# Attention scores computed a second time with the keys on the partitions, the maximum added by a product, and the sums taken as extra columns of V

## The chip, the core and the metric

The kernel runs on one core of a Trainium2 chip. The metric is the device time of one execution in microseconds (us). The engines named below are TensorE (PE; its weight loads are listed apart as PEld), VectorE (DVE), ScalarE (ACT), GpSimd (POOL) and SyncE (SP, which only issues DMAs). They run side by side and wait for each other by semaphores. PE's results go to PSUM, which the kernel allots in eight banks of 512 f32 columns on 128 partitions; DVE and ACT take them from there to SBUF.

## What is computed

Four conditional layers run one after the other on `x`, 64 sequences of 64 tokens with 256 features. Layer 0 is a feed-forward layer with quantised activations and weights, layer 1 attention and a gated feed-forward layer, layer 2 a layer norm, layer 3 an adapter whose weights differ from sequence to sequence. The change concerns the attention of layer 1, with 16 heads of 16 features:

```python
def _attention(x, W_q, W_k, W_v, W_o):
    b, l, dm = x.shape
    d_head = dm // N_HEADS
    scale = sqrt(N_HEADS / dm)                     # 0.25
    q = split(x @ W_q.T); k = split(x @ W_k.T); v = split(x @ W_v.T)
    attn = jax.nn.softmax(scale * jnp.einsum('bnqd,bnkd->bnqk', q, k), axis=-1)
    o = jnp.einsum('bnqk,bnkd->bnqd', attn, v)
    o = o.transpose(0, 2, 1, 3).reshape(b, l, dm)
    return o @ W_o.T
...
a_alpha = (t @ attn_alpha_w.T)[:, None, :]
x = x + a_alpha * _attention(_ada_rmsnorm(x, t, attn_gamma_w, attn_beta_w), W_q, W_k, W_v, W_o)
```

## The kernel before

The 4096 tokens are worked on in eight blocks (`i`) of 512 tokens, that is eight sequences. Three stretches follow each other on PE: layer 0, the attention, and the feed-forward layer with layers 2 and 3. The order of instructions on PE, DVE, ACT and POOL is the order in which the program writes them (`tc.manual_schedule`); each engine works through its own in that order, and waits come from the data and from the rotation of buffers.

The attention is the loop `for w in range(W)` (L1070) with sixteen units. Unit `w` is half `tp = w % 2` of block `i = w // 2`: four sequences, all heads. PSUM is split there into one tile `S` of four banks and four single banks `mm`, which are used in rotation. The large f32 products are made of three products of high and low parts (`mm3`, L81 to L85, type f32r); `oh`, `ol` and `xh`, `xl` are such parts.

A unit does this with its scores:

- `a_score` (L637): 32 matmuls, one for each of two pairs of sequences (`u`), two halves of the features (`m`), four groups of 32 features (`j`) and two sequences of a pair (`h`). A group of 32 features is two heads. The weights are 64 queries of `qf`, the moving operand 128 columns of `kb`: the 64 keys twice, once with the odd head's features set to zero and once with the even head's. The result has the queries on the partitions and fills the four banks of `S`.
- `a_shift` (L655), twice, each on two banks: DVE takes the maximum over 64 keys (`mx`, L660) and subtracts it (L662), which moves the scores to SBUF (`ex`).
- `a_exp` (L665), twice: ACT's exponential, in place. `a_sum` (L669), twice: DVE sums the exponentials; `a_recip` (L673) takes the reciprocals `rz`.
- `a_turn` (L683), twice: sixteen 128x128 transposes on PE (L690) put the keys on the partitions; ACT copies the four banks to `pts` (L694), DVE one of them in odd units (L692). `a_rows` (L678): ACT spreads the reciprocals to 512 columns.
- In the next unit `a_weigh` (L697): 32 matmuls with 32 columns of `vb` as weights (two heads of 16, the other one's keys set to zero) and 64 columns of `pts` moving, four side by side; ACT copies the result (L713), PE turns the spread reciprocals (L716, four transposes), DVE multiplies (L717). `a_parts` (L720): ACT makes `oh`, POOL `ol`. `a_project` (L729): the product with `W_o`, then DVE, POOL and, once a block, a DMA of POOL's queue that stores `x2`.

Between these stand pieces for the blocks to come: `todo[0]` to `todo[2]` are two value products (`a_val`) and one key product (`a_qk`) of block `i + 1` in even units and three key or query products in odd ones; `a_norm_turn` turns the normed block `i + 2` (eight transposes in even units, L256); `a_scale`, `a_begin` and `a_load` norm and load later blocks; `splits.turn` splits weights of the feed-forward layer. In the last two units `f_keep` computes the first products of that layer, and `a_turn(W - 1, 1)` to `a_project(W - 1)` stand among its first steps, after PSUM has been divided anew.

`vb` is written by four DMAs a block from `vx`, whose zeros are set once at the start (L1014).

Of the kernel before, what the change touches and what calls it, by code (L numbers as in the profile page):

```python
# [17 lines left out]
P = 128  # L18
# [18 lines left out]
def tile_kernel(ctx: ExitStack, tc, xT, x, condT, cw, upT, downT, qkvT, woT, ghT, outT_w,  # L37
# [108 lines left out]
    def cond_load():  # L146
# [6 lines left out]
        cwt = crest["w"] = pools["kv"].tile([P, TT, 2, 8, 32], F32, tag="vb", bufs=2, name="cwt")[:, :2].rearrange("p a e h d -> p (a e) (h d)")  # L153
# [4 lines left out]
    def cond_rest():  # L158
# [8 lines left out]
        nc.vector.tensor_tensor(w2, vc[:, 1, :], vc[:, 1, :], ALU.mult)  # L167
        bo = crest["bo"]
# [427 lines left out]
    def a_val(i, tp):  # L596
# [15 lines left out]
        vb = kv.tile([P, TT, 2, 8, 32], F32, tag="vb", bufs=2, name=f"vb{i}")  # L612
# [24 lines left out]
    def a_score(w):  # L637
# [15 lines left out]
        units[w] = dict(pS=pS, ex=[], pts=[], mx=pool.tile([P, 2, 32], F32, tag="mx", bufs=2, name=f"mx{w}"))  # L653

    def a_shift(w, e):  # L655

        pool, U = pools["b"], units[w]
        sv = U["pS"][:, 2 * e:2 * e + 2].rearrange("p j (a l) -> p (j a) l", l=L)
        ms = U["mx"][:, 0, 16 * e:16 * e + 16]
        nc.vector.tensor_reduce(ms, sv, AX.X, ALU.max)  # L660
        ex = pool.tile([P, 16, L], F32, tag="ex2", bufs=2, name=f"ex{w}_{e}")
        nc.vector.tensor_tensor(ex, sv, ms.unsqueeze(2).broadcast_to([P, 16, L]), ALU.subtract)  # L662
        U["ex"].append(ex)

    def a_exp(w, e):  # L665
        ex = units[w]["ex"][e]
        nc.scalar.activation(ex, ex, AF.Exp, scale=0.25)

    def a_sum(w, e):  # L669
        pool, U = pools["b"], units[w]  # L670
        nc.vector.tensor_reduce(U["mx"][:, 1, 16 * e:16 * e + 16], U["ex"][e], AX.X, ALU.add)

    def a_recip(w):  # L673
        pool, U = pools["b"], units[w]
        rz = U["rz"] = pool.tile([P, 4, 4, 2], F32, tag="rz", bufs=2, name=f"rz{w}")
        nc.vector.reciprocal(rz, U["mx"][:, 1].rearrange("p (j a h) -> p a j h", j=4, h=2))

    def a_rows(w):  # L678

        rp = units[w]["rp"] = pools["b"].tile([P, 32, 16], F32, tag="rp", bufs=1, name=f"rp{w}")  # L680
        nc.scalar.copy(rp, units[w]["rz"].rearrange("p a j h -> p (a j h)").unsqueeze(2).broadcast_to([P, 32, 16]))

    def a_turn(w, e):  # L683
        U = units[w]
        pv = U["ex"][e].rearrange("p (b h) l -> p b (h l)", h=2)
        pt = pools["b"].tile([P, 2, 512], F32, tag="pts", bufs=2, name=f"pts{w}_{e}")
        for k in range(2):
            pT = bank("mm")
            for a in range(4):
                nc.tensor.transpose(pT[:, a * P:(a + 1) * P], pv[:, 4 * k + a], ident)  # L690
            if w % 2 == 1 and k == 1:
                nc.vector.tensor_copy(pt[:, k], pT)  # L692
            else:
                nc.scalar.copy(pt[:, k], pT)  # L694
        U["pts"].append(pt)

    def a_weigh(w):  # L697

        i, tp = w // 2, w % 2
        pool = pools["b"]  # L700
        U = units.pop(w)
        pts, rp = U["pts"], U["rp"]
        po, vb = bank("po"), ablk[i]["vb"]
        for u in range(2):
            for m in range(2):
                for h in range(2):
                    o = (2 * u + m) * P + h * 64
                    for j in range(4):
                        nc.tensor.matmul(po[32 * j:32 * (j + 1), o:o + 64],
                                         lhsT=vb[:, 2 * tp + u, h, 4 * m + j, :], rhs=pts[j // 2][:, j % 2, o:o + 64],  # L710
                                         start=True, stop=True, tile_position=(0, 32 * j))
# [576 lines left out]
```

## Time and profile before

| what | value |
|---|---|
| runs | 748.68, 748.94, 749.75 us; median 748.94 |
| profiled execution, time | 748.95 us |
| profiled execution, span of the core | 746.8 us |
| granted PE clock | 1.00 |
| busy in the span: PE, DVE, ACT, POOL | 734.7 (98%), 542.2 (73%), 405.6 (54%), 340.4 (46%) us |
| layer 0 (0 to 258.5 us): PE, DVE, ACT busy | 256.4, 200.3, 123.8 us |
| feed-forward and adapter (436.7 to 746.8 us): PE, DVE, ACT busy | 303.1, 184.5, 128.3 us |
| bytes read from HBM and written to it | 71.4 and 29.6 MB |

Some groups of the attention, with the mean time of one instruction:

| group | instructions | one |
|---|---|---|
| L660 maximum, DVE, 128x1024 to 128x16 | 32 | 1220 ns |
| L662 subtraction, DVE, 128x1024 | 32 | 1225 ns |
| L671 sum, DVE, 128x1024 to 128x16 | 32 | 1214 ns |
| L667 exponential, ACT, 128x1024 | 32 | 1065 ns |
| L694 copies of `pts`, ACT, 128x512 | 48 | 621 ns |
| L692 copies of `pts`, DVE, 128x512 | 16 | 659 ns |
| L681 spreading of reciprocals, ACT, 128x512 | 16 | 667 ns |
| L713 copy of the weighed values, ACT, 128x512 | 16 | 580 ns |
| L717 product with the reciprocals, DVE, 128x512 | 16 | 677 ns |

How to read it: times of matmuls are from start to the modelled end, and matmuls overlap, so the distance between starts says what one costs. `32*64 32x128` means 32 rows and 64 columns of weights, and 32 partitions with 128 columns moving. A line such as L83 is that of a helper; the tiles' names tell which product it is.

### The profile page before, as it was taken

What the parts mean: (1) busy time and instruction counts of PE and PEld (TensorE: products, weight loads), DVE (VectorE), ACT (ScalarE), POOL (GpSimd) and SP (SyncE); (2) the same over time, 40 slices, a digit from 0 to 9 for tenths busy, and PEclk for the clock granted to TensorE, in tenths of its full rate; (3) what the DMA queues carried; (4) which work ended last, traced back from release to release, by engine and by line L of the source; (5) the groups of instructions that cost most, each with busy time, mean ns of one, the idle gap of its engine ahead of it and who ended that gap; (6) DMA issues with size and microseconds to landing.
All of it is one profiled execution on the core that took longest, in us unless ns stands there. A gap on an engine that the chain in (4) does not pass through costs nothing.

```text
span 746.8 us, 17456 instructions
## 1 busy us (share of the span) xinstructions
PE 734.7 (98%) x7036; PEld 612.1 (82%) x7036; DVE 542.2 (73%) x843; ACT 405.6 (54%) x849; POOL 340.4 (46%) x359
## 2 busy tenths in 40 slices
PE   9999999999999999999999999999999999999997
PEld 8866766777686878888888888888888888888886
DVE  4998878867687698889888876646555555565676
ACT  5553445335435588998888674535253434434242
POOL 2123133133134426765655427464646464545292
PEclk9999999999999999999999999999999999999999
DMA  8897999999995866444655237623261709080821
GB/s 258 244 265 171 270 280 231 300 278 261 229 273 108 195 153 162 113 134 122 164 150 129 79 101 183 148 52 91 63 163 32 196 4 224 1 198 2 222 62 58
DMA packets 117456, 118.87 MB, mean 159 GB/s; under 512 B 39632, under 2 KB 101200, under 8 KB 117376
## 3 DMA queue, kind: packets, MB, share of 16 engines
q1 hardware_dynamic: 109232, 91.29, 49.6%
q0 software_dynamic: 7488, 25.37, 10.9%
q10 hardware_dynamic: 656, 1.11, 0.5%
q8 instruction: 55, 0.90, 0.5%
q14 instruction: 25, 0.20, 0.1%
HBM read 71.41 MB, written 29.56 MB: 135 GB/s over the span
## 4 chain that ended last, share of the span: by engine, by line
PE 61%; DVE 17%; ACT 11%; issue 5%; DMA 3%; POOL 2%; SPq 1%; DVEq 0%; ACTq 0%; POOLq 0%
PE mm L83 9%; PE mm L85 8%; PE mm L84 8%; PE gh L85 4%; PE gh L84 4%; PE gh L83 4%; PE mm L476 3%; PE mm L298 3%; PE acc L83 2%; DMA wu<-s2d 2%; PE S L649 2%; DVE sg L799 2%; PE acc L85 2%; PE acc L84 2%; ACT x L878 2%
## 5 line engine op out<-in xcount | busy, mean ns | idle before, releaser
L83 PE MATMUL mm<-up,xhl 128*128 128x512 f32 x240 | 97.2, 405 | 0.0
L83 PE MATMUL gh<-xhf,gh 128*128 128x512 f32 x244 | 95.2, 390 | 0.0
L85 PE MATMUL gh<-xhf,gh 128*128 128x512 f32 x244 | 95.2, 390 | 0.0
L84 PE MATMUL gh<-xlf,gh 128*128 128x512 f32 x244 | 95.1, 390 | 0.0
L85 PE MATMUL mm<-up,xll 128*128 128x512 f32 x240 | 93.9, 391 | 0.0
L84 PE MATMUL mm<-up,xhl 128*128 128x512 f32 x240 | 93.6, 390 | 0.0
L799 DVE TENSOR_TENSOR sg<-gh,sg 128x512 f32<-128x512 f32 x60 | 41.3, 688 | 70.7 <-ACT sg L796 37.9
L450 ACT ACTIVATE g<-mm,rs_l 128x512 f32<-128x512 f32 x64 | 43.8, 689 | 80.6 <-PE mm L85 48.1
L837 DVE TENSOR_TENSOR hlo<-sg,hhi 128x512 fp32r<-128x512 f32 x58 | 55.2, 951 | 30.4 <-ACT hhi L836 29.5
L836 ACT CAST hhi<-sg 128x512 fp32r<-128x512 f32 x58 | 36.0, 620 | 71.9 <-DVE sg L799 71.1
L83 PE MATMUL acc<-wout,hhi 128*128 128x256 f32 x248 | 71.9, 290 | 0.0
L85 PE MATMUL acc<-wout,hlo 128*128 128x256 f32 x248 | 69.5, 280 | 0.8 <-DVE hlo L834 0.6
L451 DVE SCALAR_TENSOR_TENSOR h<-mm,rs_l,g 128x512 f32<-128x512 f32 x64 | 46.4, 744 | 32.8 <-PE mm L85 29.7
L84 PE MATMUL acc<-wout,hhi 128*128 128x256 f32 x248 | 69.3, 279 | 0.0
L260 POOL TENSOR_TENSOR xg<-xg,cv 128x512 f32<-128x512 f32 x32 | 35.3, 1114 | 71.2 <-DVE xg L259 71.2
L83 PEld LDWEIGHTS mm<-up,xhl 128*128 128x128 f32 x240 | 45.1, 188 | 15.2 <-issue 2.4
L85 PEld LDWEIGHTS gh<-xhf,gh 128*128 128x128 f32 x244 | 45.8, 188 | 9.6
L85 PEld LDWEIGHTS mm<-up,xll 128*128 128x128 f32 x240 | 45.0, 188 | 10.1
L84 PEld LDWEIGHTS mm<-up,xhl 128*128 128x128 f32 x240 | 45.2, 188 | 8.5
L83 PEld LDWEIGHTS gh<-xhf,gh 128*128 128x128 f32 x244 | 45.8, 188 | 7.3
L84 PEld LDWEIGHTS gh<-xlf,gh 128*128 128x128 f32 x244 | 45.8, 188 | 7.3
L660 DVE TENSOR_REDUCE mx<-S 128x16 f32<-128x1024 f32 x32 | 39.0, 1220 | 17.3 <-PE S L649 17.3
(220 smaller groups left out, 1929.6 us busy)
## 6 DMA issues: line engine op xcount, KB each, us to landing
gt<-in_g SPq DMA_DIRECT2D x32, 512.0 KB, 9.1
rows<-alphad SPq DMA_DIRECT2D x48, 256.0 KB, 4.8
vb<-vx SPq DMA_DIRECT2D x32, 256.0 KB, 5.1
wd<-s1d SPq DMA_DIRECT2D x32, 256.0 KB, 6.2
wu<-s2d SPq DMA_DIRECT2D x32, 256.0 KB, 6.0
xt<-in_x SPq DMA_DIRECT2D x8, 512.0 KB, 7.6
s1d<-stgs POOLq DMA_DIRECT2D x16, 256.0 KB, 8.0
s1d<-stg POOLq DMA_DIRECT2D x16, 256.0 KB, 7.9
```

The costliest lines, as they stand in the source:

```text
L83: nc.tensor.matmul(out, lhsT=l[0], rhs=r[0], start=first, stop=False)
L84: nc.tensor.matmul(out, lhsT=l[0], rhs=r[1], start=False, stop=False)
L85: nc.tensor.matmul(out, lhsT=l[1], rhs=r[0], start=False, stop=last)
L260: nc.gpsimd.tensor_tensor(b3(xg), b3(xg), bc(vb, c, i), ALU.add)
L298: nc.tensor.matmul(pb[s][c * 64:(c + 1) * 64], lhsT=gl[h], rhs=gt[h, c * GC:(c + 1) * GC], start=True, stop=True, tile_position=(64 * s, 6 ...
L450: nc.scalar.activation(g, pg, AF.Gelu, scale=rs[:, t:t + 1])
L451: nc.vector.scalar_tensor_tensor(h[:, ch * 512:(ch + 1) * 512], pv, rs[:, t:t + 1], g, ALU.mult, ALU.mult)
L476: nc.tensor.matmul(py[:, :D], lhsT=qt[:, f, :], rhs=wq[:, f, :], start=f == 0, stop=f == 7)
L660: nc.vector.tensor_reduce(ms, sv, AX.X, ALU.max)
L799: nc.vector.tensor_tensor(sg, pv, sg, ALU.mult)
L836: nc.scalar.copy(h_hi, sg)
L837: nc.vector.tensor_tensor(h_lo, sg, h_hi.bitcast(F32), ALU.subtract)
```

## The change

The exponentials are no longer turned; the scores are computed again, already turned.

- After `a_score` and the two maxima, `a_cut` splits the 32 maxima of each query into three bf16 parts (`cuts`, 24 of 32 columns of each group used).
- `a_score_turned` uses the same operands with their roles exchanged: 128 columns of `kb` are the weights, 64 queries of `qf` move, and four row groups of 32 work side by side. It writes to a new tile of the tag `S`, of which there is one, so into the four banks that `a_score` filled.
- `a_max_turn` transposes `cuts` (one bf16 transpose) and DVE copies it to `mt`. The new `a_shift` adds the negative maxima to the turned scores by 16 bf16 matmuls with the constant `sel` (entries 0 and -1) as weights. They accumulate in the same banks.
- `a_exp` reads PSUM and writes `pts` itself.
- `vx` and `vb` get two more columns for each pair of heads, one with ones at the keys of the even head, one at those of the odd head. `a_weigh` has 64 columns of `pts` as weights and 34 columns of `vb` moving, two side by side; its result has the queries on the partitions, and columns 32 and 33 are the sums of the exponentials. `a_divide` takes their reciprocals and multiplies, in two halves. The new `a_turn` turns the finished output by four transposes; ACT makes `oh` and DVE (before: POOL) `ol`.
- In the loop `a_scale`, `load_rows` and `a_load` stand before `a_score`, `a_norm_turn` turns one half in each unit instead of both in even ones, the key products of odd units have another order, and `a_project` stands at the unit's end.
- `cond_rest` builds `sel` and a bf16 identity, and POOL sets the ones in `vx` and zeros in `cuts`.

```diff
+        keys_of = main.tile([P, 8, 5], F32, tag="st", bufs=2, name="keys_of")
+        nc.vector.tensor_reduce(keys_of[:, :, 0:4], ident.rearrange("p (j c k) -> p k j c", j=4, c=4)[:, :, :, 0:3], AX.X, ALU.add)
+        nc.vector.tensor_reduce(keys_of[:, :, 4], keys_of[:, :, 0:4], AX.X, ALU.add)
+        nc.vector.tensor_scalar(pools["sel"], keys_of[:, :, 4:5].broadcast_to([P, 8, L]), -1.0, None, ALU.mult)
+        nc.vector.tensor_copy(pools["identb"], ident)
...
+    def a_max(w, e):
+        U = units[w]
+        if e == 0:
+            U["mx"] = pools["b"].tile([P, 32], F32, tag="mx", bufs=2, name=f"mx{w}")
+        nc.vector.tensor_reduce(U["mx"][:, 16 * e:16 * e + 16],
+                                U["pS"][:, 2 * e:2 * e + 2].rearrange("p j (a l) -> p (j a) l", l=L), AX.X, ALU.max)
+
+    def a_cut(w):
         pool, U = pools["b"], units[w]
-        sv = U["pS"][:, 2 * e:2 * e + 2].rearrange("p j (a l) -> p (j a) l", l=L)
-        ms = U["mx"][:, 0, 16 * e:16 * e + 16]
-        nc.vector.tensor_reduce(ms, sv, AX.X, ALU.max)
-        ex = pool.tile([P, 16, L], F32, tag="ex2", bufs=2, name=f"ex{w}_{e}")
-        nc.vector.tensor_tensor(ex, sv, ms.unsqueeze(2).broadcast_to([P, 16, L]), ALU.subtract)
...
+        mx, cuts = U["mx"].rearrange("p (j k) -> p j k", k=8), pools["cuts"][w % 2]
+        left = pool.tile([P, 4, 8], F32, tag="left", bufs=2, name=f"left{w}")
+        nc.vector.tensor_copy(cuts[:, :, 0:8], mx)
+        nc.vector.tensor_tensor(left, mx, cuts[:, :, 0:8], ALU.subtract)
+        nc.vector.tensor_copy(cuts[:, :, 8:16], left)
+        nc.vector.tensor_tensor(cuts[:, :, 16:24], left, cuts[:, :, 8:16], ALU.subtract)
+
+    def a_score_turned(w):
         i, tp = w // 2, w % 2
+        qf, kb = ablk[i]["qf"], ablk[i]["kb"]
+        pt = units[w]["pt"] = banks("S", 4)
         for u in range(2):
             for m in range(2):
                 for h in range(2):
+                    b, o = 4 * tp + 2 * u + h, (2 * u + m) * P + h * 64
                     for j in range(4):
+                        js = slice(32 * j, 32 * (j + 1))
+                        nc.tensor.matmul(pt[:, j, o:o + 64], lhsT=kb[js, m, b].rearrange("p e l -> p (e l)"),
+                                         rhs=qf[js, m, b * L:(b + 1) * L], start=o == 0, stop=False,
+                                         tile_position=(32 * j, 0))
+
+    def a_max_turn(w):
+        U = units[w]
+        pm = bank("mm").bitcast(BF16)[:, :P]
+        nc.tensor.transpose(pm, pools["cuts"][w % 2].rearrange("p j k -> p (j k)"), pools["identb"])
+        mt = U["mt"] = pools["b"].tile([P, P], BF16, tag="mt", bufs=2, name=f"mt{w}")
+        return lambda: nc.vector.tensor_copy(mt, pm)
+
+    def a_shift(w):
+        U = units[w]
+        for a in range(4):
+            for j in range(4):
+                js = slice(32 * j, 32 * (j + 1))
+                nc.tensor.matmul(U["pt"][:, j, a * P:(a + 1) * P],
+                                 lhsT=pools["sel"][js, 2 * a:2 * a + 2].rearrange("p e l -> p (e l)"),
+                                 rhs=U["mt"][js], start=False, stop=a == 3, tile_position=(32 * j, 0))
+
+    def a_exp(w, e):
+        U = units[w]
+        pts = pools["b"].tile([P, 2, 512], F32, tag="pts", bufs=2, name=f"pts{w}_{e}")
+        nc.scalar.activation(pts, U["pt"][:, 2 * e:2 * e + 2], AF.Exp, scale=0.25)
+        U["pts"].append(pts)
+
+    def a_weigh(w):
+        i, tp = w // 2, w % 2
+        U, vb = units[w], ablk[i]["vb"]
+        U["po"] = []
+        for u in range(2):
+            po = bank("mm")[:, :16 * 17].rearrange("p (n d) -> p n d", d=34)
+            U["po"].append(po)
+            for m in range(2):
+                for j in range(4):
+                    for h in range(2):
+                        o = (2 * u + m) * P + h * 64
+                        nc.tensor.matmul(po[h * 64:(h + 1) * 64, 4 * m + j], lhsT=U["pts"][j // 2][:, j % 2, o:o + 64],
+                                         rhs=vb[:, 2 * tp + u, h, 4 * m + j], start=True, stop=True,
+                                         tile_position=(0, 64 * h))
+
+    def a_divide(w, u):
+        pool, U = pools["b"], units[w]
...
+        po, rz = U["po"][u], U["rz"][:, u]
+        nc.vector.reciprocal(rz, po[:, :, 32:34])
+        nc.vector.tensor_tensor(U["of"][:, u * D:(u + 1) * D].rearrange("p (n e d) -> p n e d", n=8, e=2),
+                                po[:, :, 0:32].rearrange("p n (e d) -> p n e d", e=2),
+                                rz.unsqueeze(3).broadcast_to([P, 8, 2, 16]), ALU.mult)
+
+    def a_turn(w):
...
+            nc.tensor.transpose(pr[:, a * P:(a + 1) * P], of[:, a * P:(a + 1) * P], ident)
...
+        nc.scalar.copy(oh, pr)
         units[w, "o"] = (oh, ol)
+        return lambda: nc.vector.tensor_tensor(ol, pr, oh.bitcast(F32), ALU.subtract)
...
+        a_score(w)
+        a_max(w, 0)
+        a_max(w, 1)
+        a_cut(w)
+        if w > 0:
+            a_weigh(w - 1)
+        todo[0]()
+        a_score_turned(w)
+        max_turned = a_max_turn(w)
+        if w > 0:
+            a_divide(w - 1, 0)
+        max_turned()
+        if w > 0:
+            a_divide(w - 1, 1)
+        turned = a_norm_turn(i + 2, tp) if i + 2 <= NBLK else lambda: None
+        a_shift(w)
         a_exp(w, 0)
         if w > 0:
+            low = a_turn(w - 1)
+            low()
+        a_exp(w, 1)
         todo[1]()
+        turned()
         todo[2]()
...
+        if w > 0:
+            a_project(w - 1)
```

## The prediction

> **What bounds the kernel now.** I read the busy time by stretch first, then the matmul engine's timeline over one attention unit, then the groups by shape for prices. A unit is one of the sixteen passes of the loop over `w`; it covers four of the 64 sequences. The attention stretch runs from the first score matmul at 258.5 us to about 436.7 us.
>
> ```profile
> core 0: us, PE busy (x) PEld busy (x) DVE busy (x) ACT busy (x) POOL busy (x), PEclk, DMA share, GB/s
> 258.50:436.70 178.20, 175.24 (x2990) 151.97 (x2989) 157.43 (x178) 153.46 (x313) 101.13 (x96) 1.00 0.52 135
> ```
>
> Columns: stretch, length, then busy time and instructions of PE, PEld, DVE, ACT and POOL. PE is idle for 178.20 - 175.24 = 2.96 us in sixteen units, DVE for 20.8 us and ACT for 24.7 us. Per unit that is 9.8 us of DVE and 9.6 us of ACT in 11.1 us. All three are nearly full, but PE is fullest, and a busy PE hides small waits, so its phases have to be read from starts. One unit of PE:
>
> ```profile
> 323.84 1.21 PE L649 MATMUL S<-kb,qf 32*64 32x128 f32 x64
> 324.98 1.10 PE L709 MATMUL mm<-pts,vb 128*32 128x64 f32 x64
> 326.01 0.66 PE L716 MATMUL mm<-ident,rp 128*128 128x128 f32 x4
> 326.42 0.37 PE L83 MATMUL mm<-wv,xha 128*128 128x256 f32 x1
> ...
> 329.24 0.39 PE L83 MATMUL mm<-xha,qk 128*128 128x512 f32 x1
> ...
> 330.62 1.39 PE L256 MATMUL mm<-ident,xna 128*128 128x128 f32 x8
> 331.90 0.39 PE L83 MATMUL mm<-wo,oh 128*128 128x256 f32 x1
> ...
> 333.38 1.47 PE L690 MATMUL mm<-ident,ex 128*128 128x128 f32 x12
> 335.01 0.66 PE L690 MATMUL mm<-ident,ex 128*128 128x128 f32 x4 [0.16 <-ACT pts L694]
> 335.60 1.21 PE L649 MATMUL S<-kb,qf 32*64 32x128 f32 x64
> ```
>
> Columns: start, merged length, engine, line, tiles, shape, count. Differences of starts give the phases: scores 1.14, weighing 1.03, turning the reciprocals 0.41, value products 2.82, one key product 1.39, norm turn 1.28, output projection 1.48, turning the exponentials 2.22; together 11.76. The next unit takes 10.42 (L649 again at 346.02), so a pair averages 11.09 a unit. Every phase follows the last at once. The reader is to see that whatever is added to PE here is added to the time.
>
> **Prices on PE.** An f32 product that is not a transpose is recorded twice, so the 32 score matmuls stand as x64. What a small matmul costs can be bound by its moving columns or by the load of its weights, and the rows tell these apart.
>
> ```profile
> 83.35 2.00 PE L176 MATMUL mm<-ct,cwt 64*128 64x64 f32 x28
> 85.28 0.65 PE L180 MATMUL mm<-cwt,ct 64*64 64x256 f32 x4
> ...
> 531.36 2.04 PE L943 MATMUL mm<-x,wd 128*64 128x64 f32 x64
> 533.22 1.10 PE L959 MATMUL mm<-dn,wu 128*64 128x64 f32 x32
> ```
>
> ```profile
> L176 PEld LDWEIGHTS mm<-ct,cwt 64*128 64x128 f32 x28 | 1.9, 188 | 0.4 <-ACT junkl L232 0.4
> L709 PEld LDWEIGHTS mm<-pts,vb 128*32 128x32 f32 x1024 | 15.6, 110 | 3.3 <-issue 1.9 <-ACT rp L681 1.0 <-ACT pts L694 0.4
> L943 PEld LDWEIGHTS mm<-x,wd 128*64 128x64 f32 x448 | 13.7, 138 | 0.5 <-issue 0.4
> L476 PEld LDWEIGHTS <-qt 128*128 128x128 bf16 x256 | 23.0, 98 | 8.9 <-issue 6.7
> ```
>
> - L709 (32 weight columns, four tiles side by side, 64 moving columns): 64 records are 16 steps in 1.03 us; the starts inside stand 56 ns apart, and about 0.13 is the change of tiling.
> - L943 (64 weight columns, two side by side, 64 moving): 32 steps in 533.22 - 531.36 = 1.86 us, 58 ns a step.
> - L176 (128 weight columns, 64 moving): six pairs of row halves and two single ones, two records each, are 16 steps in 1.93 us; the starts stand 112 ns apart. Same 64 moving columns, twice the step: with 128 columns the weight load sets the pace. The loads' own times, 110, 138 and 188 ns for 32, 64 and 128 columns, rise by about 0.8 ns a column and agree.
> - A 128x128 f32 transpose (L690, L716): 109 ns between starts.
> - A change of tiling: the last start of L649 to the first of L709 is 0.20 us, of L709 to L716 0.15; about 0.1 over the step itself.
>
> **The change on PE, per unit.**
> 1. *Exponentials' turn goes.* The L690 phases sum to 33.2 us, 2.08 a unit. About 0.09 of that is the change to score tiling, which stays: **-1.99**.
> 2. *Second scores* (`a_score_turned`): 32 f32 matmuls, 64 records, on four row groups of 32 rows, 128 weight columns, 64 moving: 16 steps. At L709's step 0.90, at L176's 1.79; it has L176's columns on both sides, so I take 1.79, plus 0.19 for going into the tiling and out: **+1.98** (low end 1.09).
> 3. *Weighing turned round*: weights are now 64 columns of `pts`, moving is 34 columns of `vb`, two tiles side by side: 32 steps. L943 has the same weights and gives 32 x 58 ns = 1.86, with 0.14 of tiling 2.00. Before it was 17.5/16 = 1.09 on average. **+0.91**; if the pace followed the moving columns instead, 34 of L943's 64 would be 31 ns a step, 1.13 in all, so about 0.
> 4. *Maximum's turn and the shift by a product*: one bf16 transpose (0.05 to 0.11, by L690), then 16 bf16 matmuls in 4 steps of 56 (L709) to 112 ns (L176), each with a change of tiling in and out. The bf16 weight load of L476 takes 98 ns against 188 for f32, so I take the lower step: 0.06 + 0.03 + 0.22 + 0.22 = **+0.53** (0.45 to 0.80).
> 5. *Norm turns* are four a unit instead of eight every second: 0.47 instead of 1.28/2: **-0.17**. The four transposes of the finished output replace the four of L716: 0.
>
> Sum **+1.26 us** a unit with PE alone.
>
> [...]
>
> **What lies beside PE.** DVE loses two subtractions (1.22 each), two sums (1.21), a reciprocal (0.34), the product with turned reciprocals (0.68) and one copy (0.66), 6.6 us a unit. It gains four operations of `a_cut` on 24 or 32 columns (0.15 to 0.34 each, by the 128x1 scalar operation L458 and the reciprocal L676; I take 0.2), the copy of `mt` (0.15 to 0.41, L458 and the 128x256 copy L183; 0.25), two reciprocals and two products of `a_divide` (0.2 and 0.42), and `ol` from POOL (0.69): 3.0. ACT loses three copies of `pts`, `rp` and `of`, 3.1 us, and gains nothing: the exponential keeps its 1.06 and reads PSUM. So DVE falls to 6.3 and ACT to 6.5 us a unit; none of it shortens a unit that PE fills. Priced at nothing for that reason: all of DVE's and ACT's relief, and POOL's loss of `ol` (1.29).
>
> New waits, counting from the first score of a unit. The two maxima end at 1.25 + 2.44 = 3.7, the cuts at 4.5. PE does weighing and the first todo until 1.14 + 2.00 + 1.41 = 4.55, so the second scores, which overwrite the same four banks, don't wait; without the weighing (w = 0) they wait 1.3. `max_turn` is at 6.5; its result, the copy on DVE (0.27 + 0.25 + 0.05 us later) is covered by the four norm transposes (0.47), which leaves about 0.1. `a_divide(w-1, 1)` stands behind that copy on DVE, and `a_turn`'s third transpose waits for it: 0 to 0.2. Exponentials and `oh` on ACT end 3.0 us after the shift, PE needs the banks 4.7 us after it. At the end of odd units the last `qf` copy is behind two exponentials, a copy and a cast on ACT and ends near the next score: 0 to 0.4 per pair. Together I take 0.15 a unit (0 to 0.6, the whole round trip of `mt` uncovered).
>
> SP's loads of `at` and `ax1` are issued some 2 us earlier, POOL's x2 store some 4 us later, both a block before use; they cost nothing, and if the store were late, `f_load` would be next. Outside the loop: five DVE operations in `cond_rest` (about 1.3 us where DVE is 77% busy) and three memsets on POOL, nothing on PE; if DVE's slack were gone there, up to 1.3.
>
> **Sum.** Fifteen units x (1.26 + 0.15) = 21.2. Unit 0 loses four norm turns and waits 1.3: -0.5. After unit 15 the FFN's banks wait for the last exponential, some 2 us of PE work against 3.0 on ACT: +1.0. Total +21.7 on the profiled run, whose span is 746.8 and time 748.95, beside a median of 748.94: **770.6 us**; for this case alone 767 (no new wait, item 4 at its low end: 15 x 1.18 + 0.5) to 775 (item 4 at its high end: 15 x 1.68 + 0.5).
>
> **Rivals.**
> - *The new chain of waits decides* (score, maxima, cut, turn, copy, shift): if 0.6 to 1.1 a unit stays uncovered, 15 x 0.45 to 0.95 more: 777 to 785. For it: DVE and PE now hand over three times inside a unit. Against: the slack worked out above.
> - *Loads hide behind neighbours, columns set the pace* (the faster side): items 2 and 3 at 1.09 and 0: per unit -0.54, total about -8, **741 us**. It begins to win where the two items together cost under 1.5 us a unit (1.99 + 0.17 - 0.53, less 0.15 of waits) instead of 2.89. For it: L709 keeps 56 ns with 64 moving columns. Against: L176.
> - *Half of that* (weighing by its 34 columns, second scores by their loads): +0.35 + 0.15 a unit, **757 us**. For it: L943 has as many moving as weight columns, so it can't tell which of them sets its step.
> - *DVE or ACT was the true bound*, so that their 3 us come back: PE's 2.96 us of idle in the stretch is all there is, -3; folded into the ranges.
>
> **Chances.** Forecast 0.60, chain of waits 0.16, half 0.12, columns alone 0.08, rest 0.04 (spread). The time is the forecast's. The range 756 to 783 leaves out the columns case and the far end of the chain. Under 0.2% (1.5 us) this kernel's runs, 748.68 to 749.75, can't be told from no change: faster 0.09, same 0.02, slower 0.89.
>
> **What would show it.** In the profile of the changed kernel: the second scores' phase near 2.0 us with starts 112 ns apart (1.1 refutes item 2); weighing near 2.0 us with 58 ns steps (1.1 refutes item 3); units of 12.4 to 12.6 us; DVE and ACT near 50% busy in the stretch while PE stays over 95%. PE idle over 0.5 us a unit ahead of the shift or of the output's turn would mean the chain decides. The prediction is wrong if loads of four row groups hide behind each other's products.

## The result, and the profile after

The changed kernel takes **779.6 us** (median of four runs, 777.8 to 782.2) beside 748.9 us (748.7 to 749.8): a ratio of 1.041, 95% interval 1.037 to 1.045. The forecast was 770.6 us in a range of 756 to 783. The sign and the mechanism held; the loss is 30.7 us where 21.7 were forecast.

The profiled execution of the changed kernel took 778.25 us, its span 776.5 (before 748.95 and 746.8). I cut both spans at the first score matmul of unit 0 and of unit 15, where the work is the same, and set the three parts beside the terms of the forecast:

| part of the span | before | after | difference | forecast |
|---|---|---|---|---|
| start to first score of unit 0 (layer 0) | 258.5 | 262.8 | +4.3 | 0, up to 1.3 |
| units 0 to 14 | 164.8 | 184.4 | +19.6 | 15 x 1.41 - 0.5 = +20.7 |
| first score of unit 15 to the end | 323.5 | 329.3 | +5.8 | +1.0 |
| sum | 746.8 | 776.5 | +29.7 | +21.7 |

Busy time by stretch, as in the prediction (stretch, length, then busy us and instructions of PE, PEld, DVE, ACT and POOL, the granted clock last but two); first the kernel before, cut at the same places:

```profile
core 0: us, PE busy (x) PEld busy (x) DVE busy (x) ACT busy (x) POOL busy (x), PEclk, DMA share, GB/s
258.50:423.30 164.80, 161.89 (x2743) 140.73 (x2742) 145.99 (x164) 144.14 (x299) 97.15 (x93) 1.00 0.51 130
```

and the changed kernel:

```profile
262.80:447.20 184.40, 183.14 (x3711) 161.10 (x3711) 100.94 (x204) 107.19 (x223) 79.05 (x80) 1.00 0.47 119
447.20:776.50 329.30, 321.19 (x2962) 283.57 (x2961) 194.56 (x308) 133.45 (x274) 169.81 (x145) 0.99 0.42 106
```

DVE falls from 146 to 101 us and ACT from 144 to 107, and none of it is to be seen in the time: PE is idle for 184.40 - 183.14 = 1.3 us in fifteen units. PE issues 3711 matmul records where it issued 2743. One unit of the changed kernel on PE's timeline, with the start first:

```profile
334.31 1.21 PE L654 MATMUL S<-kb,qf 32*64 32x128 f32 x64
335.44 2.06 PE L729 MATMUL mm<-vb,pts 128*64 128x34 f32 x64
337.44 0.38 PE L83 MATMUL mm<-wv,xha 128*128 128x256 f32 x1
...
339.04 2.01 PE L689 MATMUL S<-qf,kb 32*128 32x64 f32 x64
340.99 0.23 PE L697 MATMUL mm<-identb,cuts 128*128 128x128 bf16 x1
341.06 0.61 PE L261 MATMUL mm<-ident,xna 128*128 128x128 f32 x4
341.59 0.40 PE L707 MATMUL S<-mt,sel 32*128 32x128 bf16 x16
341.93 0.67 PE L750 MATMUL mm<-ident,of 128*128 128x128 f32 x4
...
346.72 0.55 PE L654 MATMUL S<-kb,qf 32*64 32x128 f32 x19
```

The phases by differences of starts: first scores 1.13, weighing 2.00, second scores 1.95, maximum's turn 0.07, norm turn 0.53, shift 0.34, output's turn 0.42. No phase waits for another engine. The unit takes 346.72 - 334.31 = 12.41 us; units 2 to 13 take 12.35 to 12.41, 12.39 on average, where the same units before averaged 11.04 (the pair that the prediction read, 11.09): 1.35 us more. Of this, 0.31 us falls on the products of the next block and the output projection, which themselves didn't change (5.96 us a unit instead of 5.65): the changes of tiling around the new phases come to stand in them (0.21 us from the last of the first piece's products to the second scores, where two such products stand 0.11 apart). Unit 14, which has no norm turn in either kernel, takes 13.75 us instead of 11.46 and waits 0.32 us for `mt`.

### The profile page after: what moved, and what is told of

Its sections match the earlier page's. It is cut to its first block, busy times and chain, and to the rows that moved or that the text cites. A ratio compares the mean times of both kernels' runs of the same rounds, so it can differ in the third digit from the quotient of the medians.

```text
span 776.5 us, 19470 instructions
## 1 busy us (share of the span) xinstructions
PE 762.3 (98%) x8076; PEld 637.0 (82%) x8076; DVE 497.3 (64%) x894; ACT 364.7 (47%) x769; POOL 323.1 (42%) x348
## 3 DMA queue, kind: packets, MB, share of 16 engines
q8 instruction: 63, 1.03, 0.5%
## 4 chain that ended last, share of the span: by engine, by line
PE 62%; DVE 10%; ACT 6%; issue 2%; DMA 2%; SPq 1%; DVEq 0%; ACTq 0%
PE mm L83 8%; PE mm L85 8%; PE mm L84 8%; PE S L689 4%; PE mm L729 4%; PE gh L85 4%; PE gh L84 4%; PE gh L83 4%; PE S L654 2%; DMA wu<-s2d 2%; PE mm L261 2%; DVE sg L827 2%; PE acc L83 2%; PE mm L987 2%; PE mm L303 2%
## 5 line engine op out<-in xcount | busy, mean ns | idle before, releaser
L714 ACT ACTIVATE pts<-S 128x1024 f32<-128x1024 f32 x32 | 33.0, 1036 | 34.0 <-PE S L707 34.0
```

The costliest lines, as they stand in the source:

```text
L714: nc.scalar.activation(pts, U["pt"][:, 2 * e:2 * e + 2], AF.Exp, scale=0.25)
```

## The experiments

The theory: PE fills the units, and the load of f32 weights, not the moving columns, sets the pace of the small products, so that the two products the change adds or turns cost their loads. The rivals: the moving columns set the pace; the new chain of waits decides; DVE or ACT was the true bound before. Two more questions came out of the table: where layer 0 lost 4.3 us, and where the end lost 5.8.

### Half the moving columns

```
-    nc.tensor.matmul(pt[:, j, o:o + 64], ..., rhs=qf[js, m, b * L:(b + 1) * L], start=o == 0, stop=False,
+    nc.tensor.matmul(pt[:, j, o:o + 32], ..., rhs=qf[js, m, b * L:b * L + 32], start=True, stop=True,
```

> The changed kernel, but each of the second scores' matmuls moves 32 query columns instead of 64, under the same 128 weight columns and the same four tiles; the other half of the scores is left out, the table of the shift holds zeros instead of minus ones, and the shift starts its sums afresh, so the output is not attention (no stall or count of instructions differs by that). Theory 'the weight load sets the pace' (about 0.8 ns a column): starts of the second scores stay 112 ns apart, their phase stays 1.95 us, and the time stays at the changed kernel's 778 to 782 us. Rival 'the moving columns set the pace': the step falls from 112 to about 56 ns, the phase from 1.95 to about 1.05 us, the time by 15 x 0.9 = 13.5 us to about 766.

Measured: 781.1 us (778.6 to 782.4), ratio 1.043 (1.040 to 1.045). PE's timeline of this run:

```profile
338.40 1.99 PE L689 MATMUL S<-qf,kb 32*128 32x32 f32 x64
340.32 0.23 PE L697 MATMUL mm<-identb,cuts 128*128 128x128 bf16 x1
```

With 32 moving columns in place of 64 the phase is 340.32 - 338.40 = 1.92 us instead of 1.95, and nothing is gained. Moving columns don't set this pace; the rival of 766 us is out. The groups of weight loads, changed kernel (line, operation, shape and count, busy us, mean ns):

```profile
L689 PEld LDWEIGHTS S<-qf,kb 32*128 32x128 f32 x1024 | 30.1, 186 | 5.1 <-issue 3.2 <-PE mm L85 1.1
L729 PEld LDWEIGHTS mm<-vb,pts 128*64 128x64 f32 x960 | 29.2, 138 | 2.6 <-issue 2.6
```

186 and 138 ns are the 188 and 138 ns that L176 and L943 showed for 128 and 64 weight columns: the rows that the prediction chose.

### Half the weight columns

Each of the two products is cut into twice as many matmuls of half the weight columns, side by side; the two edits ran apart.

```
-    nc.tensor.matmul(pt[:, j, o:o + 64], lhsT=kb[js, m, b].rearrange("p e l -> p (e l)"), ...
-                     tile_position=(32 * j, 0))
+    for e in range(2):
+        nc.tensor.matmul(pt[64 * e:64 * (e + 1), j, o:o + 64], lhsT=kb[js, m, b, e], ...
+                         tile_position=(32 * j, 64 * e))
```

> The changed kernel, but each second-score matmul of 128 weight columns is cut into two of 64 (one for each half of the output partitions), eight tiles side by side instead of four; nothing is left out. Steps stay 16, moving columns a step stay 64. Theory 'the weight load sets the pace': a step of 64 weight columns takes about 58 ns (the row of 64 weight columns before) instead of 112, the phase 16 x 58 + 0.2 = 1.1 us instead of 1.95, a unit 11.5 instead of 12.38, the time falls by 15 x 0.85 = 13 us to about 766. Rival 'moving columns set the pace': step 112 ns, phase 1.95, time unchanged (778 to 782). Rival 'each matmul has a fixed cost at the sequencer': twice the matmuls make it longer, 128 records x 28 ns = 3.6 us, time about 800.

```
-    nc.tensor.matmul(po[h * 64:(h + 1) * 64, 4 * m + j], lhsT=U["pts"][j // 2][:, j % 2, o:o + 64], ...
+    for g in range(2):
+        q = slice(h * 64 + g * 32, h * 64 + g * 32 + 32)
+        nc.tensor.matmul(po[q, 4 * m + j], lhsT=U["pts"][j // 2][:, j % 2, o + g * 32:o + g * 32 + 32], ...
+                         tile_position=(0, q.start))
```

> The changed kernel, but each weighing matmul of 64 weight columns is cut into two of 32 queries, four tiles side by side instead of two; nothing is left out. Steps stay 32, moving columns stay 34. Theory 'the weight load sets the pace': a step of 32 weight columns with 34 moving ones can take as little as 32 ns instead of 58, the phase 32 x 32 + 0.13 = 1.15 us instead of 1.99, the time falls by 16 x 0.84 = 13 us to about 766; if a step has a floor of 56 ns (what 32 weight columns with 64 moving ones took before), the phase stays at 1.9 and the time within 2 us of 779. Rival 'moving columns set the pace': 34 columns at either cut, phase and time unchanged. Rival 'fixed cost a matmul': 128 records x 29 ns = 3.7 us, time about 806.

Measured: 788.1 us (ratio 1.052, 1.050 to 1.054) and 815.8 us (1.089, 1.084 to 1.094). Both got slower, as only the rival of a fixed cost for each matmul had said (800 and 806 us). The counts of instructions in later expectations (658, 594 and 530 a unit) are some 20 a unit too high; by the distances of the stops below either cut kernel has 640 a unit, the changed kernel so 512 (its trace has 502 and 522 loads, matmuls and waits in turn). The timeline of the first:

```profile
343.44 1.59 PE L690 MATMUL S<-qf,kb 32*64 32x64 f32 x128
344.97 0.23 PE L698 MATMUL mm<-identb,cuts 128*128 128x128 bf16 x1
...
345.57 0.39 PE L708 MATMUL S<-mt,sel 32*128 32x128 bf16 x13
346.19 0.23 PE L708 MATMUL S<-mt,sel 32*128 32x128 bf16 x3 [0.23 <-issue]
```

and of the second:

```profile
336.79 1.01 PE L731 MATMUL mm<-vb,pts 128*32 128x34 f32 x87
340.45 0.57 PE L731 MATMUL mm<-vb,pts 128*32 128x34 f32 x41 [2.65 <-issue]
...
343.30 3.69 PE L689 MATMUL S<-qf,kb 32*128 32x64 f32 x64
```

But that rival had phases of 3.6 and 3.7 us, and the products themselves are faster than in the changed kernel: the second scores take 344.97 - 343.44 = 1.53 us instead of 1.95; the weighing takes 4.16 us with a stop of 2.85 in it, 1.31 without, instead of 1.99. Not the 1.1 and 1.15 expected (the 32 ns a step behind the second rest on no row that is named there; 1.31 us over 32 steps are 41): 128 matmul records with their loads in 1.31 us are 10 ns for each pair, and in 1.53 us 12 ns, so here something other than the load has taken over. A cost per instruction would fit; no run shows it apart. And PE stops in the middle of a phase while it waits for no engine ("issue"). I listed every packet of the instruction queue beside PE's starts. Three of the stops in the second kernel:

```
stop begins   packet of 16384 bytes starts   it ends   PE goes on   instructions of PE so far
306.76        306.99                         307.87    309.55       4801
337.60        338.01                         339.04    340.45       6081
371.61        372.14                         373.08    374.63       7361
```

The stops are 1280 instructions apart, two units, and PE goes on 1.4 to 1.7 us after the packet's end. I read this as PE having run out of instructions, and call it the supply below; no run shows it more directly. (There is a packet for about 256 instructions, five for 1280: the page of the changed kernel counts 63 of them on this queue for 16,152 weight loads and matmuls, that of the second kernel 72 for 18,200.) At or after six of the seven stops of over 2 us the granted clock is 0.5 for 3.4 to 13.7 us (0.88 on average from 262 to 486 us); in one of these stretches, from 341.58 us on, L689 above takes 3.69 us instead of the 2.01 of the changed kernel. So both runs are lost to stops that neither kernel shown at the beginning has, and their times say nothing against the load. What starts a packet is open: the changed kernel issues up to 428 instructions between two of them and never stops, and the second kernel issues 428 to 435 between the packet before and the stop at six of its seven long stops.

I expected the supply to recover if the bursts were pulled apart:

```
         if w > 0:
-            a_weigh(w - 1)
+            a_weigh(w - 1, (0,))
         todo[0]()
+        if w > 0:
+            a_weigh(w - 1, (1,))
```

> The run with weighing matmuls of 32 weight columns (815.8 us, with stops of 2.8 us inside the weighing in every second unit, and half clocks after them), but the weighing's two halves stand before and after the unit's first piece of the next block instead of together; nothing is left out. Theory 'the instruction supply of PE gave out': 128 first-score and 256 weighing instructions fell into 2.5 us, while 256 of them come in one fetch; spread over 3.9 us with a piece of 24 instructions between, the stops vanish or fall under 1 us and the time falls from 816 to 768 to 780. Rival 'small weights cost more each, whatever stands around them': the weighing phases stay long and the time stays above 800.

Measured: 813.7 us (1.086, 1.084 to 1.089), a miss. Its timeline:

```profile
331.57 0.77 PE L731 MATMUL mm<-vb,pts 128*32 128x34 f32 x64
333.86 0.38 PE L731 MATMUL mm<-vb,pts 128*32 128x34 f32 x19
335.70 0.60 PE L731 MATMUL mm<-vb,pts 128*32 128x34 f32 x45 [1.45 <-issue]
...
338.78 0.39 PE L707 MATMUL S<-mt,sel 32*128 32x128 bf16 x13
342.51 0.23 PE L707 MATMUL S<-mt,sel 32*128 32x128 bf16 x3 [3.33 <-issue]
```

An undisturbed half takes 0.70 us (331.57 to 332.27 on PE's starts), both 1.40 instead of 1.99: small weights are not dear wherever they stand, and that rival is out. But the stops stay, 27.8 us in the stretch, and move: now every 1280 instructions one in the weighing and, 256 on, one in the shift. The stops follow the count of instructions, not the density of one burst as I had it.

### The sums of the kernel before

The kernel before without its two sums (`a_sum` returns at once, `a_recip` reads the maxima).

> The kernel before, with both sums of the exponentials left out (the reciprocals are taken of the maxima), so the weights are not normalised. DVE loses 2 x 1.21 us a unit, 39 us in all. Theory 'PE fills the units': time falls by at most the 2.96 us that PE was idle in the attention stretch, 746 to 749 us. Rival 'DVE or ACT was the true bound before': the time falls by 15 us or more.

Measured: 745.6 us, ratio 0.9954 (0.9937 to 0.9970). With 39 us of DVE's work gone the time falls by 3.3, about the 2.96 us that PE was idle (and 0.4 us below the range expected). DVE was not the bound before, and the 45 us that the change takes off it could bring no more than that. No run takes work off ACT alone; that ACT was not the bound either rests on PE's 2.96 us of idle time.

### The tables early

The five operations of `keys_of`, `sel` and `identb` are moved from `cond_rest` to stand ahead of `cond_norm()`.

> The changed kernel, but the five DVE operations that build the tables (keys_of, sel, identb) stand ahead of cond_norm in the kernel's idle first microseconds instead of in cond_rest in the middle of layer 0; nothing is left out. Theory 'the tables push the transposing loads and the weight loads behind them on the SP queue, and layer 0 ends late': the first score starts at 258.5 to 259.5 us (before 258.5, changed kernel 262.8), the time falls by 3 to 4 us to 775 to 777. Rival 'the late first score is scatter of the DMAs, or comes from the wider vb and the memsets': first score between 260 and 263, time unchanged within 1.5 us of 779.

Measured: 776.5 us (775.1 to 778.9), ratio 1.0373 (1.0351 to 1.0396); the interval overlaps the changed kernel's, so the trace has to speak. SP's queue in the changed kernel (one transposing load of `qt` and the weight load issued behind it, start and length):

```profile
109.72 8.32 SPq L469 DMA_TRANSPOSE qt<-q  x1
118.76 0.42 SPq L216 DMA_DIRECT2D st<-in_woT  x1
```

and with the tables early:

```profile
107.75 3.44 SPq L464 DMA_TRANSPOSE qt<-q  x1
111.92 0.42 SPq L211 DMA_DIRECT2D st<-in_woT  x1
```

With about 1.2 us of DVE's work ahead of them the transposes are issued late, one of them holds the queue for 8.3 us instead of 3.4, and the load behind it goes out at 118.8 instead of 111.9. It is no scatter: this transpose holds the queue for 6.3 to 9.3 us in all seven kernels with the tables in the middle, for 3.4 to 4.7 us in all five with the tables early, and for 4.5 us in the kernel before. Why it takes so much longer there, the runs don't show. In the changed kernel, and in the six runs above and below that keep the tables in the middle, the first score starts between 259.9 and 264.2 us; with the tables early it starts at 257.6 here, and at 258.2 to 259.3 in the four later runs (before: 258.5). So the late first score is the tables' doing; that all of it returns as time isn't shown: it is 3.1 us between medians, and of the 5.2 us that the first score gains between the two profiles only 1.8 are left at the end of the span (unit 1 is 1.0 us longer, and the part from unit 15 on 2.3 us).

### The last unit's order

In unit 15 `f_keep(2)` is moved from ahead of the second scores to behind the turn of unit 14's output.

> The changed kernel, but in unit 15 the kept FFN products f_keep(2) stand after the output's turn of unit 14 instead of ahead of the second scores; nothing is left out. Theory 'in the changed kernel PE waits 1.27 us for oh behind the first exponential, and that gap starts the half clock of 3.4 us, in which the output projection takes 3.03 instead of 1.5 us': neither the gap nor the half clock appears around 457 us, and from the last first score to the end it is 326 to 327.5 us instead of 329.3, less up to 0.9 us lost to the second scores that now wait for the maxima; time 776 to 778. Rival 'the half clock comes by its own timing': a half clock of 3.4 us stays in the stretch from 450 to 475 us and the time stays at 779.

Measured: 777.8 us (775.7 to 781.5), ratio 1.0389 (1.0363 to 1.0416), overlapping again. The changed kernel there, from PE's timeline,

```profile
456.13 0.73 PE L750 MATMUL mm<-ident,of 128*128 128x128 f32 x4
457.86 0.58 PE L83 MATMUL mm<-wo,oh 128*128 128x256 f32 x1 [1.00 <-ACT oh L753]
458.24 0.41 PE L84 MATMUL mm<-wo,oh 128*128 128x256 f32 x1
```

and its granted clock in the stretch that follows:

```profile
457.61:461.02 3.41, 3.16 (x13) 2.93 (x14) 0.69 (x1) 3.04 (x4) 0.00 (x0) 0.50 0.59 163
```

PE has nothing to cover `oh`, which ACT makes behind the first exponential; PE idles 1.00 us, and from 457.61 us on the clock is halved for 3.41 us, so that the twelve projections take 460.89 - 457.86 = 3.03 us instead of the 1.51 they take in other units. With the order changed:

```profile
450.23 2.01 PE L689 MATMUL S<-qf,kb 32*128 32x64 f32 x64 [0.55 <-DVE mx L665]
...
453.06 0.73 PE L750 MATMUL mm<-ident,of 128*128 128x128 f32 x4
453.55 0.48 PE L83 MATMUL mm<-xhf,gh 128*128 128x512 f32 x1
```

The gap and the half clock are gone, 0.55 us comes back as a wait for the maxima, and from the last first score to the end it is 773.9 - 446.5 = 327.4 us instead of 329.3, as expected. So without the gap there is no half clock here. But the gap alone doesn't make one: the same wait of 1.00 us for `oh` stands in seven kernels that keep the old order, a half clock of 3.41 us follows in six of them, and in the one with 64 weight columns in the second scores none does.

### Cheaper first scores

The first scores serve only the maxima, and a shift that numerator and sum share needn't be exact.

```
+    def high(x):
+        return x.bitcast(BF16).rearrange("p (n two) -> p n two", two=2)[:, :, 1]
...
-                         lhsT=qf[js, m, b * L:(b + 1) * L], rhs=kb[js, m, b].rearrange("p e l -> p (e l)"),
+                         lhsT=high(qf[js, m, b * L:(b + 1) * L]), rhs=high(kb[js, m, b].rearrange("p e l -> p (e l)")),
```

> The changed kernel, but the first scores, which only serve the maxima, read the upper halves of the f32 words of qf and kb as bf16 (one record for a product instead of two, half the instructions); the maxima are then those of rounded scores, the shift is the same in numerator and sum. Theory 'PE fills the units, the waits are covered': the first scores' phase falls from 1.14 to 0.5 us, a unit from 12.38 to 11.8, less what the second scores then wait for the maxima (scores, two maxima of 1.22 us and the cut need 3.8 us, and PE has 0.5 + 2.0 + 1.4 us to do): 0 to 0.2 us; the time falls by 15 x 0.4 to 15 x 0.64 = 6 to 10 us to 769 to 773. Rival 'the chain of scores, maxima, turn and shift decides the unit': the time falls by less than 3 us and the second scores wait 0.5 us or more for mx in every unit.

Measured: 768.2 us (764.9 to 768.9), ratio 1.0247 (1.0225 to 1.0269). The time is a little better than the 769 to 773 expected. The phase falls from 1.13 to 0.37 us, the unit from 12.39 to 11.64 on average (units 2 to 13), and PE's waits in units 0 to 14 are these:

```profile
PE S L692 <- DVE mx L668: 1.0, 1, 1.0
PE S L710 <- DVE mt L702: 0.3, 1, 0.3
PE mm L261 <- ACT vx L612: 0.2, 1, 0.2
```

Three single waits, 1.5 us together, the first of them in unit 0. All that PE was relieved of came back as time, so the chain of waits did not decide in the changed kernel.

### Towards a faster kernel

The next three runs hold tables early, last unit's order and cheaper first scores together (763.3 us if they add), with second scores of 64 weight columns, with exponentials and values in bf16 for the weighing (`pts`, `vb` and `vx` of type BF16), and with both.

> The changed kernel with four edits together, nothing left out: tables early, last unit's order, first scores from the upper halves, and second scores cut to 64 weight columns. The first three alone took 3.1, 1.8 and 11.4 us off the changed kernel's 779.6, together 763.3 if they add. Theory 'weight load sets the step, instruction supply stops PE when too many fall together': a unit has 64 instructions fewer than in the run that only cut the second scores (594 instead of 658); second scores 1.53 instead of 1.95 us, a unit 11.2, and 757 us if the stops vanish; up to 762 if stops of 0.45 to 0.8 us a unit stay. Rival 'a stop comes with the second scores' 256 instructions in 1.5 us whatever the rest is': stops stay as they were, 0.3 to 0.8 us a unit, 761 us or more.

> The changed kernel with tables early, last unit's order, first scores from the upper halves, and the exponentials and values kept as bf16 for the weighing (a coarser sum: each weight and value is rounded to 8 bits, in the products and in the sums alike); second scores as in the changed kernel. Theory 'the load of f32 weights, taken twice, sets the weighing's step': 32 records instead of 64 and a bf16 load of 64 columns; the weighing falls from 1.99 us to between 0.6 and 1.05, a unit from 11.6 to 10.2 to 10.7, and the time to 742 to 749, where the three other edits alone give 763. Rival 'DVE's or ACT's chain binds once PE is relieved': units stay over 11.2 us, PE waits 0.5 us or more a unit for DVE or ACT, time over 757.

> All edits together: tables early, last unit's order, first scores from the upper halves, exponentials and values as bf16 for the weighing (coarser, as in the run beside this), and second scores cut to 64 weight columns. Instructions a unit: 594 less 64 of the weighing = 530, as many as in the changed kernel, which had no stop. Theory 'supply of instructions': with no stops, second scores 1.53 instead of 1.95, a unit 9.8 to 10.3, time 736 to 743. Rival 'PE is no longer the bound there': no gain over the run beside this (within 1.5 us). If stops come back all the same (fewer microseconds for as many instructions), 743 to 750.

Measured: 769.2 us (1.028, 1.026 to 1.030), 761.9 (1.017, 1.014 to 1.019) and 758.9 (1.014, 1.012 to 1.016). The first met its rival: with 576 instructions a unit PE still stops, 10.0 us in all. The second did not reach 742 to 749 although the weighing fell from 1.99 to 0.61 us, for the waits in units 0 to 14 are now:

```profile
PE S L692 <- DVE mx L668: 7.9, 13, 0.7
PE mm L256 <- ACT vx L612: 1.7, 4, 0.7
PE mm L732 <- issue: 1.2, 1, 1.2
```

Here the rival of the prediction comes true at last: once PE was 2.1 us a unit shorter (0.76 and 1.38), the chain from first scores through two maxima to the second scores is longer than the work beside it, and PE stands still for 0.6 us in each of thirteen units. The granted clock adds to it: it is 0.5 in three stretches of 3.41 us among these units and for 10.24 us from unit 15's wait for `mx` on.

The third run met none of its three outcomes (736 to 743, 743 to 750, or no gain): it is 3.0 us faster than the second. Its thirteen waits for `mx` sum to 10.2 us, and two stops put down to "issue" to 5.3 us, though a unit has no more instructions than in the changed kernel.

The last run covers that chain: both pieces of the next block stand ahead of the second scores, both divisions ahead of the maximum's copy, and in unit 15 the output's turn ahead of the shift, in its old order otherwise.

> All edits of the fastest run so far except the last unit's order (tables early, first scores from the upper halves, bf16 exponentials and values for the weighing, second scores of 64 weight columns; 758.9 with the last unit's order), and the order inside a unit changed: the second piece of the next block stands ahead of the second scores too, both divisions ahead of the maximum's copy, and in unit 15 the turn of unit 14's output ahead of the shift. Theory 'after the edits the chain from the first scores to the maxima bounds the unit: PE waits 0.9 to 1.2 us for mx in every unit': with the piece in between, these 10 to 12 us and the half clocks after them go, a unit takes 9.8 to 10.2 us (10.99 in the kernel before), and the time is 735 to 745, below the kernel before (748.7). Rival 'the wait moves on to the exponentials or to ACT's copies': units stay at 10.9 or more, with PE waiting 0.5 us or more for ACT ahead of the next first scores, time 755 or more. If stops of the instruction supply take the gain: issue waits over 8 us in the attention stretch, time 748 to 756.

Measured: 752.1 us (751.4 to 753.6), ratio 1.0044 (1.0031 to 1.0058). Its longest waits in units 0 to 14:

```profile
PE mm L83 <- ACT xha L239: 3.1, 1, 3.1
PE mm L85 <- DVE ol L759: 1.6, 8, 0.2
PE S L657 <- issue: 1.6, 3, 1.2
PE S L693 <- DVE mx L668: 1.1, 2, 0.7
```

The wait for `mx` is gone but for 1.1 us, and units 2 to 13 take 10.2 to 11.5 us, 10.74 on average, where 9.8 to 10.2 were expected; waits for `ol` ahead of the projection (1.6 us), for ACT (3.1) and stops put down to "issue" (1.6) take part of the rest (the 3.1 us put down to ACT stand at PE's instruction 3265, where four of the other runs stop in "issue"). The time lies in the range that was given for stops of the supply, 748 to 756, but the stops are 4.7 us with that one, not the 8 that were to go with it. It comes within half a per cent of the kernel before, with coarser weights, and none of the kernels that compute the attention whole beats the kernel before.

## Why the prediction came out as it did

- **PE fills the units, and what is added to it is added to the time: right.** DVE and ACT lost 45 and 37 us in fifteen units, and nothing of it is seen to come back; PE is 99% busy there, DVE 55% and ACT 58%. The run without sums gives the bound, 3.3 us, so the rival with DVE as true bound is out; for ACT this rests on PE's idle time alone.
- **Item 1** (-1.99): the exponentials' turn is gone from the timeline as a whole. **Items 2 and 3** (+1.98 and +0.91): second scores 1.95, weighing 1.99 less 1.09 before, +0.90. Their reason, the weight load, is shown by the two cuts of the operands: half the moving columns leave the phase at 1.92, half the weight columns bring it to 1.53, and the weighing to 1.3 to 1.4 with the same 34 moving columns. The rivals "columns set the pace" and "half of that" fall with it.
- **Item 4** (+0.53) was too high: 0.07 and 0.34, +0.41. **Item 5** (-0.17) was somewhat too good: norm turn 0.53 against 0.64, -0.11. **New waits** (0.15) didn't come: in units 1 to 13 PE waits for nothing. Together units 2 to 13 became 1.35 us longer where 1.41 stood, and some luck is in that: PE's own work was put at 1.26, and the 0.15 of waits that didn't come cover the 0.09 that it lacked.
- **The sum failed at its ends.** "Five DVE operations in `cond_rest` (about 1.3 us where DVE is 77% busy) ... nothing on PE; if DVE's slack were gone there, up to 1.3" is the first step: measured 4.3 us in the profile and 3.1 between medians. I priced the operations, not what stands behind them: loads that DVE's results release, and the load behind them on SP's queue, which went out at 118.76 us, after a transpose that held the queue until 118.04.
- "After unit 15 ... **+1.0**" is the second: measured 5.8 from unit 15's first score, and the wait for banks that it stood for isn't there. The sum took fifteen units and left out the sixteenth. By its phases unit 15 is 4.9 us longer: its products cost 1.9 more, `mt` is waited for (0.5), `oh` is waited for (1.3 between starts), and the projection takes 3.0 us at half clock where it took 1.8 in the kernel before. The last weighing, 1.99 instead of 1.03, brings the other 0.9. I had worked out the cover of `mt` and `oh` for inner units alone; unit 15 has no norm turn and no next block.
- **The chain of waits as a rival** was set at 0.16 and would have given 777 to 785, where the time fell; but it is not why. The trace shows no such wait in units 1 to 13 (0.93 us for `mx` in unit 0, 0.32 for `mt` in units 14 and 15, 1.00 for `oh` in unit 15), and the cheaper first scores gave back all that PE was relieved of.

## What to carry to other kernels

Small f32 matmuls in a stream can cost what their weight loads cost: here 112 ns for each step of tiles side by side at 128 weight columns and 58 ns at 64, about 0.9 ns a column, whether 64 columns moved or half as many. At 32 weight columns that no longer holds (56 ns a step with 64 moving columns in the kernel before, 41 with 34 in the cut weighing). So look at which operand is loaded before turning a product round, and count instructions as well as nanoseconds when splitting it. Price an operation put into a phase by what its engine releases next, not by its own length, above all where loads stand behind one another on a DMA queue (here one went out at 118.8 us instead of 111.9). And follow the order of the last pass of a loop by itself: cover that every inner pass has may be missing there.

## What the runs showed of the hardware

- **PE stopped at fixed counts of instructions, beside packets of the instruction queue.** Stops of up to 4.6 us (from start to start) came at distances that are multiples of 256 PE instructions: counted in the traces from the start (weight loads, matmuls and waits), every such stop of these kernels stands at a multiple of 256 plus 193 (4801, 6081 and 7361 in the list above). A packet of 16,384 bytes on the instruction queue started within 0.6 us after the three stops listed above began, took 0.9 to 1.0, and PE went on 1.4 to 1.7 us after its end. Kernels with 640 instructions in a unit stopped in every unit or every second, one with 576 in every second; the changed kernel with 512 never stopped, but the same kernel with the tables early faltered in unit 1 at two such counts (0.42 and 0.36 us from start to start), and the two last runs with as many stopped a few times. That it is the supply is my reading of these times.
- **Cutting small matmuls in two paid less than their loads promised**: 128 matmul records with their loads took 1.31 us at 32 weight columns (10 ns each) and 1.53 us at 64 (12 ns), where 1.1 was expected of both. A floor per instruction is one reading; it wasn't tested.
- **Half clocks came in whole periods** of 3.41 us (3.4, 6.8, 10.2 and 13.7 us in these runs), and the first four of the second cut kernel lie on one grid of that period: they start at 276.73, 310.86, 341.58 and 375.71 us, 10, 9 and 10 periods apart. In the changed kernel one came with an idling of 1.00 us at 457 us, while 0.9 us in unit 0 brought none, nor did the same 1.00 us in one of seven kernels. What decides it no run shows.
